# A transformer block on one core: gate logits out of the output projection, the normalised input turned by an exchange through DRAM

## The chip, the cores and the metric

The kernel runs on one core of one Trainium2 chip. The metric is the device time of one execution in microseconds. A core has TensorE (PE, matmuls and transposes through the array), VectorE (DVE), ScalarE (ACT), GpSimd (POOL), and SyncE (SP), which here only issues DMAs; 16 DMA engines move the data.

## The reference

The input is 16 sequences of 256 tokens with 256 features, and one condition vector per sequence.

```python
shift = jax.nn.silu(t) @ W_ada.T + b_ada
h = _ln(x, ln1_g, ln1_b) + shift
qkv = (h @ Wqkv.T).reshape(b, n, 3, H, HD)          # H = 16 heads of HD = 64
q = _ln(q, qn_g, qn_b); k = _ln(k, kn_g, kn_b)      # per head
attn = jax.nn.softmax(q @ k.T / sqrt(HD))
x = x + (attn @ v) @ Wout.T
tok = x.reshape(-1, d)                              # 4096 tokens
gate = jax.nn.softmax(tok @ Wgate.T, axis=-1)       # E = 8 experts
vals, idx = jax.lax.top_k(gate.T, 4096 // E)        # each expert picks 512 tokens
g = _ln(tok[idx], mlp_g, mlp_b)
y = gelu(g @ fc1.T + b1s) @ fc2.T + b2s             # 1024 hidden
tok = tok.at[idx].add(y * vals)
```

## The kernel before

All arithmetic is in float32; a matmul of the program appears as two records in the profile. Every PE step of the attention part works on one sequence b.

**First** (per sequence): the tokens arrive as two tiles of 128 rows. VectorE takes mean and variance (L623, L625), GpSimd the reciprocal square root (L629, L106), VectorE applies both (L635, xn), PE turns the two tiles with four transposes (L659, into PSUM, ph), and ScalarE evicts them with gain and bias (L667) as hT, features on the partitions.

**Group** (six column groups of 512 for q, k and v, by two tiles): PE multiplies hT with the weights (L696, pm). For q and k ScalarE squares (L709), VectorE sums by head (L713), GpSimd takes the power (L106) and VectorE scales (L733, qk). Except in sequence 0 (`DIRECT`), the result is turned without PE: VectorE transposes 32x32 blocks (L765), SP sends them to a DRAM scratch tile (`away`, L772) and fetches them back in another order (`back`, L783), and ScalarE applies gain and bias (L789, L797). Such a pair of DMAs through DRAM is called an exchange.

**Quad** (four per sequence, four heads each): PE scores (L822, sc), VectorE maxima (L830), ScalarE exponentials (L843), GpSimd normalises (L854), and the probabilities are turned: by an exchange (L864 transpose, L872 away, L885 back into prT), or, for the quads in `OFFS`, by PE transposes (L891, pp) and a ScalarE copy (L898). Before the change `OFFS` holds all four quads of sequence 0 and the last two of sequence 15. PE multiplies with v (L910, po), ScalarE evicts (L925, oT).

**Tail** (two tiles per sequence): PE projects oT with `wo` in eight accumulating matmuls (L936, pw); VectorE adds the residual (L943, tok) and normalises it again for the experts; SP stores both to DRAM (L947, L957). For the gate PE transposes tok twice (L962, pg), ScalarE copies it (L968, tokT), PE multiplies with the gate weights (L973, pl) and VectorE copies the 8 logits (L979, gates).

**Routing**: with the gates of sequences 0 to 14, a bitwise search of 30 steps finds each expert's threshold; each step is a VectorE comparison (L1101), a small PE count (L1110, pc) and a VectorE choice (L1125). Sequence 15's last work and filler transposes (L557) stand between the steps. Then the lists of tokens are made (L1154 to L1254).

**Jobs**: 16 expert jobs of 256 tokens each (8 experts, two rounds): load weights (L1211 to L1216), gather tokens, two matmul layers (L1333, L1353), scatter-add to the output.

The order of the instructions up to the first job's end is written out by hand: each step is declared once with its engine, and the list `PLACES` gives every step a number; the steps are issued in the order of these numbers.

```python
def order(self, places):
    assert len(places) == len(self.steps)
    return sorted(range(len(places)), key=lambda k: (places[k], k))
```

Every engine works through its own instructions in that order, and waits at one whose input or buffer isn't ready. SP is one such queue: a DMA that waits there holds those behind it.

Of the kernel before, what the change touches and what calls it, by code (L numbers as in the profile page):

```python
# [9 lines left out]
F32 = mybir.dt.float32  # L10
I32 = mybir.dt.int32
BF16 = mybir.dt.bfloat16
AF = mybir.ActivationFunctionType
# [53 lines left out]
def kernel(  # L67
# [6 lines left out]
    woutT: bass.AP,  # L74
    wgateT: bass.AP,
# [76 lines left out]
    def make_others():  # L152
# [21 lines left out]
    DIRECT, OFFS = (0,), {(b, d) for b in (0, B - 1) for d in range(HP // 2)} - {(B - 1, 0), (B - 1, 1)}  # L174
# [11 lines left out]
        0, 0, 3.75, 4.52, 3.3, 4.02, 4.42, 7.76, 0.23, 0, 8, 9.39, 23.39, 15.62, 11.2, 13.11,  # L186
        20.2, 18.21, 0, 0, 0, 0, 0, 0, 0, 3.5, 4.21, 5.54, 5.02, 5.73, 6.59, 7.1, 7.76, 10.88,
        12.83, 14.5, 15.29, 17.61, 24.11, 24.82, 14.6, 16.55, 19.6, 20.39, 22.79, 26.35, 27.24,
        12.61, 14.56, 17.01, 17.93, 21.59, 25.9, 26.57, 18.4, 20.35, 22.19, 22.98, 25.11, 26.8,
        27.91, 22.38, 24.33, 29.19, 31.14, 27.46, 29.41, 30.12, 30.98, 32.96, 34.54, 35.93, 30.92,  # L190
        32.87, 33.58, 34.37, 36.58, 49.98, 53.03, 35.14, 39.48, 40.19, 43.73, 45.71, 48.98, 49.77,
        37.37, 39.98, 40.79, 41.85, 43.83, 49.5, 51.4, 39.1, 41.05, 47.25, 49.28, 32.65, 34.78,
        36.6, 38.11, 40.83, 41.54, 34.18, 34.97, 39.02, 41.27, 42.03, 37.84, 42.73, 33.67, 35.38,
        37.56, 40.03, 41.71, 42.52, 35.98, 38.52, 40.94, 42.15, 43.01, 39.76, 45.64, 46.88, 43.75,
        44.99, 45.78, 51.95, 55.85, 56.57, 46.91, 50.44, 52.86, 56.29, 57.06, 51.68, 58.63, 44.77,
        46.31, 47.37, 53.77, 61.53, 62.58, 47.51, 52.07, 54.68, 65.43, 66.15, 53.31, 66.89, 68.13,
        56.73, 58.17, 58.96, 65.08, 73.25, 73.97, 61.18, 63.07, 69.75, 75.42, 76.14, 64.31, 80.95,
        57.76, 59.98, 61.13, 63.26, 75.86, 76.63, 59.38, 60.17, 64.17, 78.03, 78.74, 62.99, 79.93,
        82.15, 65.87, 67.71, 68.62, 72.43, 89.64, 90.45, 67.11, 69.58, 71.52, 88.18, 88.9, 71.25,
        92.4, 78.91, 80.39, 81.19, 88.14, 94.44, 95.25, 84.26, 85.77, 89.05, 90.23, 94.21, 87.01,  # L200
        99.51, 101.48, 112.85, 116.83, 117.98, 117.98, 119.21, 119.72, 119.79, 120.23, 125.51,
        126.28, 116.32, 120.15, 122.66, 121.3, 122.16, 123.66, 125.96, 127.43, 132.51, 133.33, 0,
        15.1, 17.17, 27.27, 12.59, 13.3, 24.78, 46.66, 48.33, 50.66, 53.7, 54.41, 55.59, 57.57,
        58.77, 54.12, 56.07, 56.78, 59.35, 61.78, 63.16, 52.39, 54.34, 55.05, 57.47, 60.58, 62.38,
        63.18, 64.54, 67.74, 69.34, 74.46, 61.97, 64.03, 64.74, 65.99, 68.31, 69.1, 69.9, 71.34,
        74.54, 76.14, 80.34, 59.65, 62.09, 67.91, 70.54, 63.7, 65.65, 66.36, 67.87, 69.85, 70.64,
        69.79, 71.74, 72.45, 73.34, 75.32, 76.11, 71.52, 73.47, 74.18, 75.22, 77.32, 78.11, 78.91,
        80.27, 83.47, 85.07, 89.39, 73.69, 75.64, 76.72, 77.51, 79.79, 80.99, 81.79, 83.15, 86.35,
        87.95, 93.36, 76.3, 78.25, 82.84, 87.23, 81.82, 83.66, 84.81, 86.32, 87.38, 83.06, 83.85,
        87.23, 88.59, 86.05, 89.39, 90.75, 93.95, 95.55, 104.14, 88.62, 89.86, 90.94, 93.72,  # L210
        95.37, 90.46, 91.9, 94.63, 95.98, 93.34, 96.78, 98.14, 101.34, 102.94, 108.93, 114.54,
        93.42, 94.77, 95.74, 103.48, 104.54, 96.59, 101.97, 104.39, 106.35, 103.21, 107.15,
        108.51, 111.73, 113.93, 127.28, 98.49, 99.73, 100.52, 105.3, 109.36, 100.33, 102.93,
        106.21, 110.57, 104.17, 111.37, 112.73, 116.16, 118.36, 128.3, 129.49, 105.16, 107.56,
        108.71, 114.78, 117.83, 106.96, 107.75, 112.05, 116.22, 111.78, 122.3, 124.9, 128.1,
        129.97, 139.32, 106.18, 108.76, 111.12, 112.96, 114.39, 108.16, 110.16, 113.87, 115,
        112.55, 115.8, 117.16, 120.7, 122.9, 138.3, 140.41, 109.95, 112.72, 115.03, 120.22,
        125.07, 111.95, 113.58, 119.31, 129.55, 119.04, 130.35, 131.97, 135.17, 136.77, 142.08,
        121.74, 123.27, 124.06, 126.71, 130.68, 123.87, 125.02, 127.62, 128.94, 126.44, 131.48,
        133.17, 136.77, 138.77, 143.1, 145.7, 159.6, 163.6, 164.95, 164.75, 166, 166.55, 173.78,  # L220
        174.91, 176.32, 177.22, 163.07, 167.2, 168.65, 168.35, 170.41, 172.99, 176.77, 179.56,
        180.45, 181.22, 0, 26.23, 27.18, 28.97, 25.71, 26.42, 27.6, 78.47, 79.23, 84.72, 86.73,
        87.99, 89.96, 91.94, 92.73, 86.45, 88.4, 89.2, 91.84, 94.17, 97.19, 90.67, 92.86, 93.57,
        95.54, 97.8, 99, 99.8, 101.16, 104.36, 106.14, 112.08, 95.03, 96.98, 98.4, 99.19, 101.17,
        101.96, 102.94, 104.94, 108.14, 109.74, 115.99, 96.76, 103.89, 107.05, 109.67, 100.53,
        104.88, 105.75, 107.12, 109.97, 115.61, 102.41, 104.38, 105.15, 109, 111.18, 121.15,
        110.97, 113.08, 113.79, 115.69, 118.44, 119.54, 120.34, 121.7, 124.9, 126.5, 132.75,
        120.01, 121.96, 122.67, 123.46, 125.68, 126.61, 127.41, 128.77, 131.97, 134.37, 139.02,
        123.63, 126.94, 129.17, 131.31, 122.76, 127.74, 128.53, 132.16, 133.49, 124.47, 125.98,
        133.07, 134.7, 131.89, 138.37, 140.77, 143.97, 145.57, 155.83, 126.26, 128.34, 130.35,  # L230
        138.22, 139.83, 131.29, 135.85, 139.13, 140.44, 137.09, 141.24, 142.6, 145.8, 147.57,
        154.81, 156.92, 131.49, 132.73, 133.75, 136.4, 148.24, 134.1, 134.89, 137.31, 147.02,
        136.13, 149.04, 150.99, 154.95, 157.79, 171.89, 140.19, 142.03, 142.82, 145.91, 156.57,
        141.43, 143.78, 146.82, 153.56, 145.64, 157.37, 159.79, 162.99, 164.59, 172.91, 175.21,
        141.21, 143.23, 144.74, 154.31, 160.52, 145.04, 149.04, 151.52, 159.91, 150.28, 161.39,
        163.39, 167.05, 168.99, 185.54, 149.31, 150.55, 151.34, 158.04, 161.73, 154.17, 154.96,
        158.95, 162.34, 157.18, 164.59, 166.59, 169.79, 171.39, 184.52, 188.07, 150.33, 152.35,
        157.41, 160.92, 170.74, 154.77, 158.37, 160.01, 169.8, 159.74, 174.92, 177.12, 180.72,
        182.72, 190.02, 156.7, 157.94, 162.28, 165.51, 175.49, 159.14, 161.32, 166.42, 171.95,
        165.2, 176.29, 178.32, 182.68, 185.92, 191.04, 192.13, 198.43, 202.27, 204.54, 203.47,  # L240
        204.66, 207, 215.16, 215.88, 216.4, 217.76, 206.68, 210.37, 212.02, 212.16, 213.19,
        216.86, 213.06, 216.18, 222.5, 223.22, 0, 28.45, 29.46, 48.11, 26.75, 27.94, 48.44,
        131.05, 131.8, 133.11, 137.31, 138.12, 140.04, 142.63, 143.83, 134.84, 136.81, 137.52,
        141.92, 144.44, 146.41, 136.57, 138.52, 139.23, 143.8, 145.81, 147.63, 148.43, 149.79,
        152.99, 154.59, 159.33, 145.85, 147.8, 148.85, 149.64, 151.75, 152.95, 154.59, 156.59,
        159.79, 161.39, 165.59, 143.97, 146.19, 153.08, 155.92, 147.58, 150, 151.15, 152.43,
        155.97, 162.99, 151.2, 153.3, 155.37, 156.16, 158.54, 166.59, 157.72, 160.33, 161.13,
        161.92, 164.6, 165.39, 166.19, 167.79, 171.39, 173.39, 179.86, 166.54, 168.49, 169.2,
        169.99, 172.56, 173.76, 174.56, 175.92, 179.12, 180.72, 184.92, 168.27, 170.22, 174.59,
        176.65, 170, 173.16, 173.95, 178.17, 179.23, 171.35, 172.14, 179.08, 180.61, 177.71,  # L250
        182.32, 184.72, 187.92, 189.52, 195.52, 171.02, 174.37, 178.1, 180.11, 181.38, 176.1,
        177.14, 181.02, 182.59, 179.84, 184.92, 187.92, 191.12, 192.72, 212.04, 214.1, 182.63,
        185.36, 186.15, 193.17, 194.4, 184.76, 187.11, 192.26, 193.79, 190.79, 196.32, 198.54,
        205.4, 207.74, 219.75, 183.65, 190.19, 190.98, 194.08, 195.61, 187.17, 189.06, 194.99,
        196.22, 192.22, 197.02, 199.74, 202.94, 204.54, 218.73, 221.32, 196.54, 198.38, 199.53,
        202.56, 203.88, 197.78, 198.57, 201.65, 203.27, 201.38, 205.04, 206.54, 214.9, 217.74,
# [1455 lines left out]
```

## Time and profile before

| | us |
|---|---|
| median of three runs | 1073.79 (1072.8 to 1074.13) |
| the profiled execution | 1073.31 |
| its span, first to last instruction | 1071.6 |
| PE busy | 1036.4 (97%) |
| VectorE busy | 825.5 (77%) |
| GpSimd busy | 617.2 (58%) |
| ScalarE busy | 589.6 (55%) |
| token transposes on PE (L962), busy | 12.7 |
| input transposes on PE (L659), busy | 10.1 |
| gate products on PE (L973), busy | 17.5 |
| projections on PE (L936), busy | 115.2 |

The mean granted TensorE clock is 0.988. Busy times of PE overlap: a record lasts until its modelled end, and the next has begun by then. In the profile a line such as `pw<-wo,oT` reads "pw is written from wo and oT", with the shape and the number of records; "idle" and "wait" name the engine and line that released the waiting instruction.

### The profile page before, as it was taken

The page shows a single profiled execution, that of the slowest core. Times are in us where ns is not written, and L with a number is a line of the kernel's source. Part 1 is how long each engine was busy: PE and PEld are TensorE (multiplying, and loading weights), DVE is VectorE, ACT ScalarE, POOL GpSimd, SP SyncE. Part 2 cuts the span into 40 slices and gives each one's busy share as a digit, 9 for nine tenths or more (in the row PEclk, how much of TensorE's full clock was granted, in tenths as well). Part 3 has the DMA queues.
Part 4 walks back from the last instruction along what each step waited for, and adds up shares of the span by engine and source line. Part 5 has one row for each costly group of instructions (what it writes and reads, how often), then busy time and mean ns, then how long its engine had stood idle before and what let it go on. Part 6 is the DMA issues. An engine that isn't in the chain of part 4 may idle for free. (4 is left out here: it accounts for less than half of the span.)

```text
span 1071.6 us, 17747 instructions
## 1 busy us (share of the span) xinstructions
PE 1036.4 (97%) x5519; PEld 677.5 (63%) x5519; DVE 825.5 (77%) x2295; ACT 589.6 (55%) x1646; POOL 617.2 (58%) x997
## 2 busy tenths in 40 slices
PE   7899999999999999999999999999788999999996
PEld 4455656555555655556566565666477888888885
DVE  6667888989888898798888888888667588656530
ACT  1577676676666666575766667675503323333231
POOL 3666776778767686667767686675401423343332
PEclk8999999999999999999999999999999999999999
DMA  6014889888987898887888888899430656667772
GB/s 218 1 60 158 272 290 324 290 290 283 308 274 264 285 317 311 289 289 262 287 301 289 290 296 292 291 316 309 167 102 22 184 146 188 197 189 203 232 236 30
DMA packets 169710, 250.53 MB, mean 234 GB/s; under 512 B 9744, under 2 KB 139536, under 8 KB 169616
## 3 DMA queue, kind: packets, MB, share of 16 engines
q1 hardware_dynamic: 161696, 239.11, 65.8%
q0 software_dynamic: 6144, 8.39, 4.3%
q10 hardware_dynamic: 1776, 1.90, 0.5%
q8 instruction: 44, 0.72, 0.3%
q14 instruction: 50, 0.41, 0.1%
HBM read 142.67 MB, written 106.69 MB: 233 GB/s over the span
## 5 line engine op out<-in xcount | busy, mean ns | idle before, releaser
L696 PE MATMUL pm<-wq,hT 128*128 128x512 f32 x768 | 362.1, 609 | 6.7 <-DVE qk L733 2.5
L854 POOL TENSOR_SCALAR pr<-pr,sums 128x256 f32<-128x256 f32 x512 | 238.2, 486 | 97.2 <-DVE sums L850 90.1
L843 ACT ACTIVATE pr<-sc,nmax 128x256 f32<-128x256 f32 x512 | 237.8, 481 | 102.0 <-DVE nmax L830 81.3
L696 PEld LDWEIGHTS pm<-wq,hT 128*128 128x128 f32 x768 | 138.3, 191 | 162.2 <-issue 138.0
L106 POOL TENSOR_TENSOR ss<-ss,neghalf 128x8 f32<-128x8 f32 x128 | 210.7, 1646 | 10.7
L830 DVE TENSOR_REDUCE nmax<-sc 128x2 f32<-128x512 f32 x256 | 165.7, 676 | 13.8 <-PE sc L822 13.1
L864 DVE STREAM_TRANSPOSE pb<-pr 128x512 f32<-128x512 f32 x232 | 154.1, 687 | 7.4 <-POOL pr L854 6.9
L822 PE MATMUL sc<-kT,qT 64*128 64x256 f32 x1024 | 135.2, 394 | 0.0
L910 PE MATMUL po<-prT,v 128*64 128x256 f32 x1024 | 128.8, 389 | 2.7 <-DMA prT<-blocks 2.7
L709 ACT ACTIVATE sq<-pm 128x512 f32<-128x512 f32 x128 | 76.8, 604 | 89.7 <-PE pm L696 87.3
L1370 POOL DMA_INDIRECT out<-y,idx x32 | 50.9, 1592 | 122.7 <-DVE oh L1246 57.1
L822 PEld LDWEIGHTS sc<-kT,qT 64*128 64x128 f32 x1024 | 91.3, 186 | 46.9 <-issue 28.5
L1333 PE MATMUL ph<-xT,w 128*128 128x256 f32 x512 | 116.8, 383 | 0.9 <-ACT xT L1318 0.9
L936 PE MATMUL pw<-wo,oT 128*128 128x256 f32 x512 | 115.2, 381 | 0.0
L1353 PE MATMUL py<-w,hid 128*128 128x256 f32 x512 | 115.1, 380 | 0.0
L910 PEld LDWEIGHTS po<-prT,v 128*64 128x64 f32 x1024 | 66.9, 137 | 68.5 <-issue 19.9
L936 PEld LDWEIGHTS pw<-wo,oT 128*128 128x128 f32 x512 | 96.3, 190 | 21.0 <-issue 6.0
L843 ACT ACTIVATION_READ_ACCUMULATOR pr<-sc,nmax 128x1 f32 x512 | 108.2, 211 | 0.0
L733 DVE TENSOR_TENSOR qk<-pm,ss 128x512 f32<-128x512 f32 x128 | 89.7, 702 | 23.8 <-POOL ss L106 21.5
L1353 PEld LDWEIGHTS py<-w,hid 128*128 128x128 f32 x512 | 96.1, 190 | 13.2
L1333 PEld LDWEIGHTS ph<-xT,w 128*128 128x128 f32 x512 | 95.0, 190 | 14.9 <-ACT xT L1318 2.4
L713 DVE TENSOR_REDUCE ss<-sq 128x8 f32<-128x512 f32 x128 | 85.1, 670 | 22.1 <-ACT sq L709 20.5
(144 smaller groups left out, 1050.6 us busy)
## 6 DMA issues: line engine op xcount, KB each, us to landing
blocks<-pb SPq DMA_DIRECT2D x116, 512.0 KB
prT<-blocks SPq DMA_DIRECT2D x116, 512.0 KB
kblocks<-kb SPq DMA_DIRECT2D x60, 512.0 KB
w<-in_fc2T SPq DMA_DIRECT2D x16, 1024.0 KB
qraw<-kblocks SPq DMA_DIRECT2D x30, 512.0 KB
kT<-kblocks SPq DMA_DIRECT2D x30, 512.0 KB
w<-in_fc1T SPq DMA_DIRECT2D x9, 1024.0 KB
w<-in_fc1Q SPq DMA_DIRECT2D x7, 1024.0 KB
```

Of the source, the lines that this page charges most:

```text
L106: nc.gpsimd.tensor_tensor(dst, src, neghalf[:, : src.shape[1]], ALU.pow)
L696: nc.tensor.matmul(self.pm, hTs[self.b][:, c, bass.ts(self.t, P)], wq[:, c, bass.ts(self.g, GW)], start=(c == 0), stop=(c == DC - 1),)
L733: engine.tensor_tensor(dst, src.rearrange("p (q e d) -> p q e d", q=QB, e=8), by_head(self.ss[:, 1, :]), ALU.mult,)
L822: nc.tensor.matmul(self.sc[i, j][:, t, :], qTs[self.b][rows, hp, bass.ts(t, P)], keys[rows, hp] if whole else keys[rows, hp // 4, hp % 4], ...
L830: nc.vector.tensor_reduce(self.nmax[i, j], self.sc[i, j], AX.X, ALU.max, negate=True)
L843: nc.scalar.activation(dst, src, AF.Exp, bias=self.nmax[i, j][:, t : t + 1], scale=1.0, accum_out=self.sums[i][:, 0, j, t : t + 1],)
L854: nc.gpsimd.tensor_scalar(self.pr[i, j][:, t, :], self.pr[i, j][:, t, :], self.sums[i][:, 1, j, t : t + 1], 1.0, ALU.mult, ALU.mult,)
L864: nc.vector.transpose(self.pb[i][:, :, :, j].rearrange("p k c t n -> p t k c n"), self.pr[i, j].rearrange("p t (k c m) -> p t k c m", c=TB ...
L910: nc.tensor.matmul(self.po[j * HD : (j + 1) * HD, i, :], vs[self.b][:, c, bass.ts(4 * self.d + 2 * i + j, HD)], prT[:, j, c] if (self.b, s ...
L936: nc.tensor.matmul(self.pw, oTs[self.b][:, hp // 2, self.t, hp % 2, :], wo[:, hp, :], start=(hp == 0), stop=(hp == HP - 1),)
L1333: nc.tensor.matmul(self.ph[f], self.w1[:, c, bass.ts(f, P)], self.xT[:, :, c].rearrange("p k i n -> p k (i n)") if self.exchanged else sel ...
L1353: nc.tensor.matmul(self.py[i], self.hid[:, f, bass.ts(i, P)], self.w2[:, f, :], start=(f == 0), stop=(f == FC - 1),)
```

## The change

**Gate.** With tok = x + o Wout.T, the logits are tok Wgate.T = x Wgate.T + o (Wgate Wout).T. A new step `Fold` loads Wout once more, multiplies it with the gate weights on PE and writes the result as 8 more columns of `wo`, so that the projection is 264 columns wide. Two small matmuls add the part of x, for which x is loaded a second time, transposed on the host (`xT`, one buffer, one load per sequence). The token transposes, their copy and the separate gate product are gone; the logits are copied out of pw.

**Input.** Except in sequence 0 (`XDIRECT`) the normalised input is turned by an exchange: ScalarE applies mean and reciprocal deviation (with an offset that GpSimd makes), VectorE transposes 32x32 blocks, SP sends and fetches, ScalarE applies gain and bias. The weights are permuted on the host to match.

**Quads.** (0, 2) and (0, 3) leave `OFFS`: their probabilities go by exchange.

**Weights of the first jobs.** Their loads come behind the first step of the routing (`"turned"`). **Order.** `PLACES` is new as a whole, and the costs written beside the steps are changed (they have no effect in the kernel, which takes only the order from `PLACES`).

```diff
-    DIRECT, OFFS = (0,), {(b, d) for b in (0, B - 1) for d in range(HP // 2)} - {(B - 1, 0), (B - 1, 1)}
+    DIRECT, OFFS = (0,), {(b, d) for b in (0, B - 1) for d in range(HP // 2)} - {(B - 1, 0), (B - 1, 1), (0, 2), (0, 3)}
+    EXCHANGED = (0, 1, 2, 3)
+    XDIRECT = (0,)
...
-        wo = attw.tile([P, HP, D], F32, name="wo")
+        wo = attw.tile([P, HP, D + E], F32, name="wo")
...
+        def load_xT(b):
+            xTs[b] = seq.tile([P, DC, N], F32, tag="xT", bufs=1, name=f"xT{b}")
+            nc.sync.dma_start(
+                xTs[b], xT[:, b * N : (b + 1) * N].rearrange("(c p) n -> p c n", p=P)
+            )
+
+        class Fold:
+            def load(self):
+                self.w = seq.tile([P, DC, H * HD], F32, tag="oT", bufs=2, name="wout")
+                nc.sync.dma_start(self.w, wout.rearrange("(c p) f -> p c f", p=P))
+
+            def product(self):
+                self.pf = ps.tile([P, HP, E], F32, tag="mm", bufs=3, name="pf")
+                for hp in range(HP):
+                    for c in range(DC):
+                        nc.tensor.matmul(
+                            self.pf[:, hp], self.w[:, c, bass.ts(hp, P)], wg[:, c],
+                            start=(c == 0), stop=(c == DC - 1),
+                        )
+
+            def evict(self):
+                nc.scalar.copy(wo[:, :, D:], self.pf)
...
+            def offset(self):
+                nc.gpsimd.tensor_scalar(
+                    self.rs[:, 0:1], self.mv[:, 0:1], self.rs[:, 1:2], -1.0, ALU.mult, ALU.mult
+                )
...
+                    nc.scalar.activation(
+                        dst, src, AF.Identity, bias=self.rs[:, 0:1], scale=self.rs[:, 1:2]
+                    )
...
+            def turn(self, t):
+                if t == 0:
+                    self.xb = work.tile([P, QB, DC, TB, SQ], F32, tag="qk", bufs=3, name="xb")
+                nc.vector.transpose(
...
+            def away(self):
+                self.blocks = dram.tile([QB, SQ, QB, P], F32, tag="xblocks", bufs=2, name="xblocks")
...
+            def back(self):
+                self.raw = work.tile([P, QB, DC, TB, SQ], F32, tag="sq", bufs=2, name="xraw")
...
+            def affine(self):
+                b = self.b
+                hTs[b] = seq.tile([P, DC, N], F32, tag="hT", name=f"hT{b}")
+                for c in range(DC):
+                    nc.scalar.activation(
+                        hTs[b][:, c].rearrange("p (t k n) -> p k t n", t=TB, k=QB),
+                        self.raw[:, :, c], AF.Identity,
...
-            def project(self, a=0, b=HP):
-                if a == 0:
-                    self.pw = ps.tile([P, D], F32, tag="mm", bufs=3, name="pw")
-                for hp in range(a, b):
+            def project(self):
+                self.pw = ps.tile([P, D + E], F32, tag="mm", bufs=3, name="pw")
+                for hp in range(HP):
                     nc.tensor.matmul(
                         self.pw, oTs[self.b][:, hp // 2, self.t, hp % 2, :], wo[:, hp, :],
-                        start=(hp == 0), stop=(hp == HP - 1),
+                        start=(hp == 0), stop=False,
+                    )
+                for c in range(DC):
+                    nc.tensor.matmul(
+                        self.pw[:, D:], xTs[self.b][:, c, bass.ts(self.t, P)], wg[:, c, :],
+                        start=False, stop=(c == DC - 1),
                     )
...
-            def transposes(self):
-                self.pg = ps.tile([P, D], F32, tag="mm", bufs=3, name="pg")
...
-            def evict(self):
-                self.tokT = work.tile([P, D], F32, tag="tokT", name="tokT")
...
-            def gate(self):
-                self.pl = ps.tile([P, E], F32, tag="po", name="pl")
...
-                nc.vector.tensor_copy(gates[:, self.n, :], self.pl)
+                nc.vector.tensor_copy(gates[:, self.n, :], self.pw[:, D:])
...
-        at(-999, "ACT", 0.3, later_loads)
+        at(-999, "ACT", 0.3, later_loads, ["sT"])
...
-            at(ROUTE + 60 + n * 80, "SP", 1.5, jobs[n].load, (), [("w", n)], [("oT", B + n), ("v", B + n)], lag=6.0)
+            at(ROUTE + 60 + n * 80, "SP", 1.5, jobs[n].load, ["turned"], [("w", n)], [("oT", B + n), ("v", B + n)], lag=6.0)
```

## The prediction

> **What bounds the kernel now.** I read the busy times and slices of the page first, to see where which engine is full.
>
> ```profile
> span 1071.6 us, 17747 instructions
> ...
> PE 1036.4 (97%) x5519; PEld 677.5 (63%) x5519; DVE 825.5 (77%) x2295; ACT 589.6 (55%) x1646; POOL 617.2 (58%) x997
> ...
> PE   7899999999999999999999999999788999999996
> ...
> DMA  6014889888987898887888888899430656667772
> ```
>
> TensorE (PE) is full from slice 3 to 28, has a dent at slices 29 to 31 (the routing) and is full again in the expert stage; the DMA engines are nearly as full in the attention stage, at 8 or 9 tenths. A busy PE is modelled, so I asked next for the whole attention stage as one window (PE, PEld, DVE, ACT, POOL busy, then clock, DMA share, GB/s), and for what made PE wait inside it.
>
> ```profile
> 55.00:757.00 702.00, 701.35 (x3436) 404.04 (x3434) 598.16 (x1193) 472.41 (x1396) 493.25 (x849) 1.00 0.82 279
> ```
>
> ```profile
> PE pl L973 <- DVE gates L979: 0.4, 1, 0.4
> PE pm L696 <- ACT hT L667: 0.2, 1, 0.2
> ```
>
> These two lines are all the PE waits of 702 us: 0.6 us. VectorE has 104 us to spare there, ScalarE 230, GpSimd 209. So in this stage a microsecond of PE work is a microsecond of the span, until something else takes over. Prices must be steps of PE, not means of overlapping records, so I read them from the timeline of PE as the distance from one start to the next.
>
> ```profile
> 448.05 3.72 PE L936 MATMUL pw<-wo,oT 128*128 128x256 f32 x16
> 451.61 1.88 PE L696 MATMUL pm<-wq,hT 128*128 128x512 f32 x4
> 453.32 0.38 PE L962 MATMUL pg<-ident,tok 128*128 128x128 f32 x2
> 453.54 1.88 PE L696 MATMUL pm<-wq,hT 128*128 128x512 f32 x4
> 455.26 0.51 PE L973 MATMUL pl<-wg,tokT 128*128 128x8 f32 x4
> 455.70 2.00 PE L822 MATMUL sc<-kT,qT 64*128 64x256 f32 x16
> ...
> 459.50 0.66 PE L659 MATMUL ph<-ident,xn 128*128 128x128 f32 x4
> 460.00 1.88 PE L696 MATMUL pm<-wq,hT 128*128 128x512 f32 x4
> ```
>
> One projection (pw) takes 3.56 us, the two token transposes (pg) 0.22 here and 0.28 at the other tile of this sequence, a gate product (pl) 0.44, the four input transposes (ph) 0.50.
>
> **The change, part by part.** All on PE first, over 16 sequences of two tiles.
>
> Removed: pg, 32 tiles by 0.27 us (12.7 us busy in the groups over 64 records is 0.40, but records overlap; the starts over the whole stage give 0.22 to 0.28, mean 0.27): -8.7. ph, 15 sequences by 0.50: -7.5 (sequence 0 keeps them). Two quads of sequence 0 go from PE transposes (pp) to the exchange: 32 transposes; 16 of them start at 48.18 and the next step at 50.02, so 0.115 each: -3.7. Their four exchanges meet a DMA at 0.16 to 0.45 (slices 3 and 4), and VectorE's eight transposes of 0.69 its gaps there: 0.
>
> Added: the projection's rows go from 256 to 264 columns, 3.56 x 8/256 = 0.11 per tile, 32 tiles: +3.5 (ends: 0, if 8 columns hide in the issue, and 7, if they cost double). The gate product stays, as two matmuls with x transposed instead of the token transposed: same shapes, same 0.44, so 0 (it loses its own waits, 0.4 us, and its tokT copy). The fold is 16 matmuls with 8 columns, two records each, 32 at pl's 0.11 a record: +3.5 once, at the start, where PE has 11 us of gaps before 54 us (the first two slices); between 0 (in a gap) and 7 (with a slow clock: the first slice had 0.80). I take all of 3.5.
>
> Sum on PE: -8.7 - 7.5 - 3.7 + 3.5 + 3.5 = -12.9. The last sequence's two tiles are projected in the routing stage, where PE is not the bound: 2 x (0.27 - 0.11) = 0.3 is not on the path. **-12.6 us.** I compared the two written-out orders as lists: up to the last projection of sequence 14, which the routing waits for, both put the same 192 QKV groups, 126 score steps and 120 products on PE, so no work moves across that point, and PE changes mode about as often (255 and 254 times, some 0.1 us each).
>
> Other engines, per sequence. VectorE: two applies of 0.43 leave, two 128x256 transposes of 0.45 come (the row xb<-xg, L1296): nothing. ScalarE: two tokT copies (0.38) and two evictions (0.58) leave, two applies (0.38 to 0.58 by the 128x256 rows) and two affines (0.59) come: +0.2 of 15 free. GpSimd: two offsets of 0.2: +0.4 of 13 free. SP issues three more DMAs, 0.3 to 0.4 us each. All lie under PE. If that cover were gone they would cost 0.6 a sequence.
>
> DMA is the tight one. In 107 to 750 us:
>
> ```profile
> q1 hardware_dynamic: 124550, 187.34, 85.9%
> ```
>
> That is 552 us of 16 engines for 187 MB, 2.95 us per MB. The first projections of sequences 0 and 14 start at 120.50 and 743.68, 44.5 us per sequence, so 38.2 us of DMA in each. New are the away and the back of the normalised input and x transposed, 256 KB each, 0.79 MB: 2.3 us, together 40.5. PE's period falls by 0.54 + 0.50 - 0.22 = 0.82 to 43.7. DMA goes from 86% to 93%. Does PE start to wait there? The nearest rows:
>
> ```profile
> 160.74:187.53 26.79, 26.79 (x128) 16.55 (x127) 23.51 (x51) 17.62 (x53) 18.45 (x34) 1.00 0.97 324
> 375.06:401.85 26.79, 26.79 (x132) 14.36 (x132) 25.23 (x47) 18.41 (x52) 22.85 (x36) 1.00 0.94 317
> 735.00:763.00 28.00, 25.52 (x167) 17.86 (x165) 21.41 (x56) 19.24 (x67) 15.30 (x34) 1.00 0.95 331
> ```
>
> At 0.97 and 0.94 in mid-stage PE never idled; at 0.95 at the end, with little other work to put before a late product, it did. Ends: 0, and (below) +25. Mid-stage is the nearer row: I take +1.
>
> The Trainium skill's page "DMA: Bandwidth & Descriptors" (Bandwidth, Rules for kernel authors) speaks against small transfers: batch to 1 MiB or more, 0.95 us for 64 KB and 6.15 us for 1 MB. On a line between them, as an estimate, 256 KB takes 2.0 us and the three 6.0, and DMA would need 44.2 us per sequence, over PE's 43.7. The trace disagrees so far: its transfers of 512 KB and less cost 2.95 us per MB.
>
> The added waits. The x-transposed load has one buffer, so SP waits at it until the sequence before is projected, and behind it on SP stand the aways and backs of the next quads; the order puts it right behind that projection, so I count 0. The input's exchange adds two DMA trips before the QKV groups; the nearest rows are those of the expert stage, in the chain of waits:
>
> ```profile
> 967.85 2.62 DMA xblocks<-xb
> 970.53 2.84 DMA xT<-xblocks
> ```
>
> 5.5 us, more under load; the new order has the affine at least one full QKV step and mostly several ahead of its first reader, so 0. It borrows a qk and an sq buffer for that time, which PE's groups need; at 3 and 2 buffers against some 7 us in 43.7 I count 0 and leave it to the +1. The wait of the early loads for the silu changes nothing: they are issued at 7.30, behind it (4.24), already.
>
> End of attention and routing. With pg and pl gone there is less to put between the last exchanges of sequence 14 and its products: a prT wait, +1.5 (0 to 4). On the other side the first job's weights, issued at 741.62 to 744.21 in the middle of those exchanges, now go behind the routing's first transpose. The waits there:
>
> ```profile
> PE pc L1110 <- DVE reach L1101: 5.9, 11, 0.8
> PE po L910 <- DMA prT<-blocks: 2.7, 3, 1.1
> ```
>
> Of the 2.7 I take -1. The second job's load now comes first, so the first job's may be the one that waits for a buffer of the last projection, as the second one's does now (issued at 794.15, when that projection ends; its bytes are through 10 us later). That projection now stands just before the totals, and from the totals (804.37) to the first expert matmul (819.97) are 15.6 us: it lands under the routing's end, 0; without those 5 us to spare it would cost up to that. The last projection moves from between two routing steps to just before the totals: +0.5.
>
> Total: -12.6 + 1 + 1.5 - 1 + 0.5 = **-10.6 us**. The profiled execution took 1073.31 us (span 1071.6 and 1.7 around it), which gives 1062.7; the median of the three runs is 0.5 above it, so I forecast 1063.
>
> **Rivals.**
> (1) Part of the gain is absorbed: the start (chains, not PE, set it, and the fold and ScalarE's applies for sequences 1 to 4 sit in it) gives back 3 to 5 us and the others 2 more: 1069. For it: PE has those 11 us of gaps, which no PE saving touches. Against: only the fold and one sequence's transposes are there.
> (2) Slower: the exchanges come late to their products. Place: po<-prT; price: the three waits at 759 to 765 us, 0.9 each; a sequence saves 0.82, so it decides from one late product in eight per sequence. At three, 14 x 2.7 = 38 less the 10.6: 1100; at two, 1088. For it: DMA at 93%, one queue on SP, one more wait in it. Against: 0.97 was borne for 27 us without a wait.
> (3) DMA occupancy is the bound: if each of the three new transfers takes 2.0 us of the 16 engines (three quarters of the landing times above), DMA needs 44.2 a sequence, 0.5 over PE's period: 14 x 0.5 = 7 of the gain is lost, 1070. The Trainium skill's rule above gives this time. Against it stands 2.95 us per MB.
> (4) It comes to nothing: the 8 extra columns and the fold cost double (+7) and prT waits of 4 more, the end's upper bound, take the rest: 1073.
>
> **How the numbers follow.** Forecast 0.66 (own range 1058 to 1067); (1) 0.10; (3) 0.05; (2) 0.15; (4) 0.04. About 0.2% (2.1 us) is what a measurement here can tell from no change. Faster: 0.66 + 0.10 + 0.05 = 0.81; same 0.04; slower 0.15. Low end: fold in the gaps (-3.5) and all prT waits gone (-1.7): 1057. High end: (1), (3), (4) and the beginning of (2), one late product in each sequence, 14 x 0.9 = 12.6 on the 1062.7: 1076.
>
> **What would show it.** Right: PE work in the attention stage 12 to 13 us less, pg gone, ph with 4 records, pw near 3.67 plus 0.44 a tile; PE waits on prT under 3 us there; DMA 0.90 to 0.95; sequence 14 projected some 11 us earlier. Wrong: rows PE po <- DMA prT with tens of waits, or pw at more than 4.2 us a tile with its gate part, or a first expert matmul not earlier than 812.

## The result

The changed kernel takes 1078.22 us (median of 20 runs, 1074.11 to 1083.36), the kernel before 1073.72 (20 runs, 1071.31 to 1077.81): ratio 1.0044, 95% interval 1.0033 to 1.0054, so 4.5 us slower. In a later comparison the ratio was 1.0027 (1.0013 to 1.0041, 10 runs). The forecast was 1063.

The profiled execution took 1075.04 us, near the lower end of those runs, with a span of 1073.3 against 1071.6 of before. So the profile shows 1.7 of the 4.5 us. First the page after: busy PE, then its 40 slices, then those of the DMA engines.

```profile
span 1073.3 us, 17620 instructions
...
PE   6899999999999999999999999998979999999996
...
DMA  7017899999999888999898899997603656666772
```

DMA has moved up to 8 and 9, as expected. The dent of the routing is a slice earlier, but not followed by anything that ends earlier. The attention stage as one window and PE's longest waits in it (engine and line, what it waited for, us in total, times, longest):

```profile
55.00:757.00 702.00, 696.77 (x3312) 391.40 (x3311) 599.39 (x1199) 473.83 (x1386) 503.74 (x880) 1.00 0.88 299
```

```profile
PE sc L910 <- ACT kT L885: 1.8, 1, 1.8
PE sc L910 <- DVE nmax L918: 1.7, 1, 1.7
...
```

With three shorter rows the waits come to 5.2 us, from 0.6, and none of them is the prT wait that the prediction watched for. The prices of the steps and the DMA share came out near what was worked out: a projection with its gate part takes 3.66 + 0.37, and the queue holds the 16 engines for 90.3% of 107 to 750 us (85.9% before, 93% forecast).

```profile
442.55 3.83 PE L1023 MATMUL pw<-wo,oT 128*128 128x264 f32 x16
446.21 0.51 PE L1028 MATMUL pw<-wg,xT 128*128 128x8 f32 x4
446.58 1.96 PE L784 MATMUL pm<-wq,hT 128*128 128x512 f32 x4
```

Where the time went is seen at the two ends of the stage. At the start, from the timelines of before and then of after, ScalarE's issues of QKV weights (before all three, after the last two) and PE's first QKV step:

```profile
7.74 3.11 ACTq L590 DMA_DIRECT2D wq<-in_wqkvT  x3
...
11.60 7.64 PE L696 MATMUL pm<-wq,hT 128*128 128x512 f32 x12 [0.51 <-ACT hT L667]
```

```profile
7.70 1.75 SPq L583 DMA_DIRECT2D wout<-in_wout  x1
9.99 0.37 ACTq L627 DMA_DIRECT2D wq<-in_wqkvT  x1
16.36 0.37 ACTq L627 DMA_DIRECT2D wq<-in_wqkvT  x1
...
17.48 6.99 PE L784 MATMUL pm<-wq,hT 128*128 128x512 f32 x12 [6.90 <-ACT hT L755]
```

SP sends Wout (1 MB) and the first x transposed out at 7.7 and 10.7 us, behind the first loads. The order names a need for the fold's load, the third sequence's statistics, but only its plan knows of it: the DMA itself reads and overwrites nothing that is in use, so SP doesn't wait for it. From the start of its first weight issue to the end of its third ScalarE needs 8.14 us instead of 3.11, and the eviction of hT behind them on ScalarE comes 5.9 us later, with it the first QKV step.

An issue by itself takes 0.37 to 0.51 us; the time goes by ahead of the third, 6.0 us after the second. There ScalarE waits for a semaphore, the counter that tells of a DMA's landing. In the records of these traces the first DMAs of SP and ScalarE use eight semaphores together, and from the ninth on an issue starts 0.02 us or more after the DMA that had its semaphore before has landed. Before, the third weight load has the semaphore of another weight load, landed at 10.45 us, and is issued at 10.47. After, the two added loads take two semaphores, the third weight load gets that of `wo` (1 MB), landed at 16.34, and is issued at 16.36.

At the other end, PE's timeline after, where little but sequence 15's scores is left:

```profile
734.35 2.12 PE L910 MATMUL sc<-kT,qT 64*128 64x256 f32 x16
738.15 0.70 PE L910 MATMUL sc<-kT,qT 64*128 64x256 f32 x2 [1.67 <-DVE nmax L918]
739.06 1.13 PE L910 MATMUL sc<-kT,qT 64*128 64x256 f32 x6 [0.21 <-ACT pr L931]
742.01 2.08 PE L910 MATMUL sc<-kT,qT 64*128 64x256 f32 x8 [1.82 <-ACT kT L885]
744.02 3.68 PE L998 MATMUL po<-prT,v 128*64 128x256 f32 x16
```

The last QKV matmul starts at 729.0, where before has one at 738.0. Then score steps stand one behind the other, PE waits for VectorE's maxima, for ScalarE's exponentials and longest for kT, which ScalarE finishes at 741.96 behind eight exponentials, and two product steps that take 1.88 us elsewhere take 3.6: the granted clock is 0.81 in 736:744 and 0.77 in 744:752, where before has 1.00 in both.

The span's difference by stages (start of the first QKV step; end of the last gate product that the routing needs; the routing's first transpose; first expert matmul), with the kernels of the experiments:

| kernel | QKV | gates | routing | experts | span | median | ratio to before (95%) |
|---|---|---|---|---|---|---|---|
| before | 11.6 | 755.0 | 760.3 | 820.0 | 1071.6 | 1073.7 | 1 |
| after | 17.5 | 756.8 | 760.9 | 820.2 | 1073.3 | 1078.2 | 1.0044 (1.0033 to 1.0054) |
| e1_hold | 11.5 | 752.0 | 756.1 | 814.5 | 1067.5 | 1073.9 | 0.9999 (0.9982 to 1.0016) |
| e2_before_early | 17.3 | 758.4 | 762.9 | 823.3 | 1075.2 | 1076.4 | 1.0026 (1.0014 to 1.0038) |
| f1_fill_hole | 11.7 | 751.7 | 755.8 | 815.8 | 1068.0 | 1069.9 | 0.9964 (0.9950 to 0.9978) |
| f3_no_exchange_early | 10.8 | 757.5 | 761.7 | 822.3 | 1074.9 | 1076.6 | 1.0033 (1.0022 to 1.0044) |
| f4_end_order | 10.9 | 746.3 | 749.4 | 811.4 | 1064.6 | 1066.4 | 0.9947 (0.9926 to 0.9968) |
| g1_split_last | 11.4 | 750.1 | 753.2 | 808.7 | 1061.6 | 1062.6 | 0.9919 (0.9887 to 0.9950) |
| g2_weights_back | 12.2 | 751.4 | 755.4 | 820.5 | 1075.0 | 1074.8 | 1.0015 (0.9998 to 1.0031) |

The ratios are to runs of before on the same chip (1072.6 to 1074.0 there). The stages are of one execution each; e1, profiled twice, differs by 4 us in them, so a stage's difference of a few us is only believed where the medians say the same.

### The profile page after: what moved, and what is told of

Same layout as the page of the kernel before. It is cut to its first block, busy times and chain, and to the rows that moved or that the text cites. A ratio compares the mean times of both kernels' runs of the same rounds, so it can differ in the third digit from the quotient of the medians.

```text
span 1073.3 us, 17620 instructions
## 1 busy us (share of the span) xinstructions
PE 1032.2 (96%) x5395; PEld 668.4 (62%) x5395; DVE 825.4 (77%) x2303; ACT 590.6 (55%) x1637; POOL 625.5 (58%) x1027
## 5 line engine op out<-in xcount | busy, mean ns | idle before, releaser
L108 POOL TENSOR_TENSOR ss<-ss,neghalf 128x8 f32<-128x8 f32 x128 | 210.9, 1648 | 10.7
L952 DVE STREAM_TRANSPOSE pb<-pr 128x512 f32<-128x512 f32 x240 | 158.0, 685 | 10.3 <-POOL pr L942 5.6
L998 PE MATMUL po<-prT,v 128*64 128x256 f32 x1024 | 131.0, 391 | 0.1
L1023 PE MATMUL pw<-wo,oT 128*128 128x264 f32 x512 | 122.4, 393 | 0.0
L1406 PE MATMUL ph<-xT,w 128*128 128x256 f32 x512 | 116.8, 383 | 2.4 <-ACT xT L1391 2.4
L1406 PEld LDWEIGHTS ph<-xT,w 128*128 128x128 f32 x512 | 95.0, 190 | 16.4 <-ACT xT L1391 3.7
```

The lines of the kernel that those rows point to most:

```text
L108: nc.gpsimd.tensor_tensor(dst, src, neghalf[:, : src.shape[1]], ALU.pow)
L952: nc.vector.transpose(self.pb[i][:, :, :, j].rearrange("p k c t n -> p t k c n"), self.pr[i, j].rearrange("p t (k c m) -> p t k c m", c=TB ...
L998: nc.tensor.matmul(self.po[j * HD : (j + 1) * HD, i, :], vs[self.b][:, c, bass.ts(4 * self.d + 2 * i + j, HD)], prT[:, j, c] if (self.b, s ...
L1023: nc.tensor.matmul(self.pw, oTs[self.b][:, hp // 2, self.t, hp % 2, :], wo[:, hp, :], start=(hp == 0), stop=False,)
L1406: nc.tensor.matmul(self.ph[f], self.w1[:, c, bass.ts(f, P)], self.xT[:, :, c].rearrange("p k i n -> p k (i n)") if self.exchanged else sel ...
```

## The experiments

**The start.** The theory: the early 1.25 MB is what delays the first QKV step. One kernel holds it back, the other gives it to the kernel before.

```diff
 class Fold: def load(self):
     self.w = seq.tile([P, DC, H * HD], F32, tag="oT", bufs=2, name="wout")
+    nc.vector.memset(self.w[:, :, 0:1], 0.0)
     nc.sync.dma_start(self.w, ...)
```

> The changed kernel, with one VectorE memset into the tile of Wout ahead of its load, at the load's place in the order, so that the 1 MB really waits until some 20 us and does not go out behind the first loads. Theory 1 (the early 1.25 MB fills the queues, ScalarE stands 5 us longer in issuing its three wq loads and hT comes late): first QKV matmul back from 17.5 to 11.6 +- 0.4 us, ScalarE's three issues back from 8.1 to about 3 us, time 5 to 6 us less than the changed kernel's 1078.2, so 1072 to 1073.5. Rival (the start is late because of the new order or of the wait for the silu): first QKV matmul stays at 17 to 17.5, time 1077 to 1079.

Measured: first QKV step at 11.49, median 1073.9, 0.4 us over the expected range. ScalarE's issues end at 10.75, as those of before do (10.85). The third weight load again has the semaphore of another weight load (landed at 10.30, issued at 10.32).

```diff
 for b in (3, 4): load_x(b)          # before.py, last_loads
+early = seq.tile([P, DC, H * HD], F32, tag="oT", ...); nc.sync.dma_start(early, wout...)
+early = seq.tile([P, DC, H * HD], F32, tag="oT", ...); nc.sync.dma_start(early[:, :, :N], xT...)
```

> The kernel before, with the loads of Wout (1 MB) and of x transposed of sequence 0 (0.25 MB) put behind its first loads on SP, into tiles that nobody reads; nothing else changed. Theory 1: first QKV matmul at 16 to 17.5 instead of 11.6 us, time 4 to 6 us over the 1073.7 of before: 1077.7 to 1079.7. Rival (the late start belongs to the order): 1073.5 to 1074.5, first QKV matmul at 11.6 to 12.

Measured: first QKV step at 17.30, as in the changed kernel; median 1076.4, 1.3 us under the expected range, because of the 5.7 us lost at the first step 2.3 are won back on the way to the gates. Both say the same: the early loads cost 2.4 to 4.3 us, in either order. The rival falls. Here too the third weight load stands behind `wo`: `wo` is issued at 4.38, the view of its tile gives

```profile
L604 SPq DMA_DIRECT2D wo<-in_woutT x1: 538/538/538, 4.4 to 4.4; - x1
DMA to landing us min/median/max: 11.8/11.8/11.8
```

so it lands at 16.16, and the third weight load is issued at 16.18. So the loads do not simply fill the queues, as the theory had it. In e1 `wo` lands at 14.90: by that, as an estimate, some 4.5 of the 5.9 us come from the change of semaphore (10.47 to 14.9) and the rest from the added bytes. No run takes the two apart.

**The middle: the input's exchange, and the fold alone.** Between the stage's ends PE has many more gaps of some 0.1 us. Theory 2 put them down to the exchange.

```diff
-XDIRECT = (0,)
+XDIRECT = tuple(range(B))    # with e1's memset; e4: ph 0.9 us ahead of the first QKV step in the order, f3: 3.6
```

> e1 with the input's exchange undone: VectorE applies, PE transposes (ph, 15 x 0.50) and ScalarE evicts as before, just ahead of each sequence's first QKV group; the rest of the new order stands. Theory 2 (the exchange makes the small gaps, some 11 us): +7.5 of ph, -9 to -11 of gaps: 1 to 4 us less than e1, about 1070. Rival 2b (the new order makes the gaps, or the fold): +7 to +8 over e1, about 1080.

Measured: 1091.2, ratio 1.0159 (1.0125 to 1.0193): neither. The order that I wrote put the eviction too close to its reader:

```profile
PE pm L750 <- ACT hT L721: 8.3, 13, 0.7
```

So it prices a bad place, not the exchange, and was run again with more room.

> e4 again, the input's exchange undone on top of e1, but with the four transposes and the eviction put 3.6 us of the order ahead of the first QKV group (more for three sequences), so that nothing waits for hT. Theory 2b (the exchange is worth the 15 x 0.50 = 7.5 us of its transposes and costs nothing in waits): 7 to 9 us over e1. Rival 2 (the exchange gives part of it back in small waits): 3 to 6 us over e1.

Measured: 1076.6. By the ratios that is 3.6 us over e1 (some 2 either way): rival 2. Where the other half of the 7.5 us went is not settled. Against e1's first profile the small gaps are not the exchange's: the distances from start to start, summed by tile from the first QKV step to the gates, are the same in f3 and e1 (QKV 358.1 and 358.0, scores 131.4 and 131.1, products 116.8 and 117.6), though f3 has no exchange of the input and its 15 sequences' transposes take 7.85. But that was e1's fastest run. Its second profile (below), near its median as f3's is, has 360.5, 132.5 and 118.5, 5.2 us more than f3 in these three, so by that one the exchange does give back part of its gain in small waits.

```diff
-OFFS = ... - {(B - 1, 0), (B - 1, 1), (0, 2), (0, 3)};  XDIRECT = (0,);  PLACES = those of after
+OFFS = ... - {(B - 1, 0), (B - 1, 1)};  XDIRECT = tuple(range(B));  PLACES = those of before, step by step
```

> The fold alone, in the order of before: gate columns in the output projection, x transposed loaded behind each sequence's last projection, Wout's load held back as in e1, the fold's product at 46 us of the order; the input transposes stay on PE, the two quads of sequence 0 keep theirs, the first jobs' weights stay where they were. By the steps of PE: token transposes -8.2, gate products -1.8, 8 columns +3.2, fold +3.6, so -3.2: 1070.5. Theory 2 (the small gaps of some 0.1 us on PE, 16 us before and 28 us after the change, come from the input's exchange and its closer waits): gaps stay at 16 to 18 us and the time is 1069.5 to 1071.5. Rival 2a (they come from the x transposed and the DMA traffic it adds): gaps over 22 us, time 1074 or more.

Measured: 1090.8, ratio 1.0156 (1.0140 to 1.0172): theory 2 missed by far, and rival 2a's "1074 or more" holds only as a number. The steps have the forecast prices, but the order of before without its token transposes and gate products runs into waits, the first line in 55:757, the second in 757:782:

```profile
PE pm L749 <- DVE qk L786: 4.1, 6, 1.1
```

```profile
PE po L963 <- DMA prT<-blocks: 4.8, 4, 1.7
```

The removed steps had covered other chains. A hand-written order with steps taken out is another order, so this run doesn't price the fold.

**The hole at the end of attention.** Theory 3: what the middle gains is lost in the hole at 732 to 746 us. f1 only fills it, f4 takes it away.

```diff
+at(729.75, "PE", 1.7, partial(fill_mm, 16), ...)   # fill_mm: fill with its tile in "mm"
+at(734.3, "PE", 1.3, partial(fill_mm, 12), ...)
+at(736.0, "PE", 0.9, partial(fill_mm, 8), ...)
```

> e1 with 36 identity transposes of no use put on PE into the hole at the end of attention (16 behind the first score step of sequence 15's second quad, 12 behind the next, 8 behind the one after; 0.11 us each). In e1's profile PE idles there from 732 to 740 us and its granted clock falls to 0.62 in 736:744. Theory 3 (the hole costs twice: the waits, and a lower clock afterwards whose place and length vary from run to run, which is why the median of e1 lies 4.6 us over its profiled run): clock 1.00 in those windows, the product behind the hole back from 3.06 to 1.95 us, median 2 to 4 us under e1's 1073.9, spread of the runs narrower than e1's 8.6 us. Rival 3a (the low clock is harmless, the scores wait for ScalarE anyway): median within 1 us of e1.

Measured: 1069.9, 4.0 under e1's median (3.8 by the ratios), with 36 matmuls of no use added; spread 5.9 us. One window of e1, then of f1 (columns as above):

```profile
736.00:744.00 8.00, 6.74 (x35) 3.58 (x34) 5.15 (x11) 5.67 (x21) 4.49 (x10) 0.62 0.49 165
```

```profile
736.00:744.00 8.00, 7.64 (x60) 5.27 (x57) 5.78 (x13) 6.71 (x25) 4.69 (x11) 1.00 0.63 213
```

The product behind the hole is back from 3.06 to 1.95 us. So the low clock is not harmless, and rival 3a falls. How much of the 4.0 it is, the profiles leave open: from sequence 13's last projection to sequence 14's first f1 takes 25.1 us, e1 26.2 and, in its second profile, 27.0. The Trainium skill's page "TensorE: Matmul & The Clock Gate" (Part 1, What's actually happening) says that PE falls to half its clock after an idle window of about 3.4 us, and that this window runs free of the kernel; the trace agrees with a fall, since 0.62 lies between half and full, but not with that length: e1's longest idle stretch in the hole is 1.67 us. No run here shows that the window runs free.

f4 gives all engines another order from 688 us on. On PE, from the first projection of sequence 13:

```diff
-pw13.0 pm pm sc14.3 po pm po sc14.3 pw13.1 pm pm po po sc15.0 po po sc15.0 sc15.1 (hole) sc15.1 (hole) sc15.2
+pw13.0 pm pm pm sc14.3 sc14.3 po po pw13.1 sc15.0 po po pm sc15.0 sc15.1 pm po sc15.1 po sc15.2
```

> e1 with the last 60 us of attention in another order on all engines: the last projection of sequence 13, the two last value groups and the scores of sequence 15 are spread so that PE never waits for a score buffer; in the order's own times the holes of 3.7 and 0.9 us at 730 us become one of 1.0 and the routing's first transpose comes 4.2 us earlier. Theory 3 (the hole at the end of attention is where the middle's gain goes): routing's first transpose 4 to 7 us earlier than e1's 756.1, no clock under 0.9 between 728 and 756 us, median 4 to 7 us under e1: 1067 to 1070. Rival 3b (the end is set by the exponentials and exchanges of sequence 15, whatever the order of PE): routing's start within 1.5 us of e1's, 1072.5 to 1074.

Measured: 1066.4, 7.5 under e1 by the medians (of six runs) and 5.6 by the ratios (some 3 either way); the routing's first transpose at 749.4 against 756.1; clock 1.00 from 728 to 752. Rival 3b falls: the end was set by the order.

**The routing.** In f4 the last projection stands between the last threshold count and the totals. g1 cuts both projections of sequence 15 into pieces behind sixteen counts.

```diff
-def project(self):
+def project(self, a=0, z=HP):      # one hp per piece; the gate part with the last
-at(p, "PE", 4.07, a.project, ...)
+for z in range(HP): at(p + z, "PE", 0.45 if z < HP - 1 else 0.9, partial(a.project, z, z + 1), ...)   # b == 15
```

> f4 with the two projections of sequence 15 cut into eight pieces of 0.45 us each (the last with the gate part 0.9), one piece behind each of the sixteen threshold counts from 20 to 5 of the routing, where PE is free for some 0.9 us per count; the tail of the first of them on VectorE and the first job's weights behind it move along. In f4 they stand as blocks: 4.1 us between two counts, where a count takes 1.0, and between the last count (789.8) and the totals (795.9), 6.1 us where before had 1.0. Theory 4 (the last projection moved ahead of the totals costs 3 to 5 us and not 0.5): last count to first expert matmul back from 21.7 to 16 to 18 us, first expert matmul 5 to 7 us earlier than f4's 811.4, median 1060 to 1062. Rival 4a (VectorE's chain or the weights' landing set the start of the experts): 1065 to 1067.

Measured: 1062.6. The medians of f4 and g1 stand on six runs each and their intervals overlap; the profiles are clearer, f4's last count and what follows, then g1's:

```profile
789.78 0.16 PE L1182 MATMUL pc<-cnt,twice 128*128 128x1 bf16 x1
789.80 5.85 PE L1022 MATMUL pw<-wo,oT 128*128 128x264 f32 x16
...
795.85 0.16 PE L1226 MATMUL po<-tot,below 128*128 128x1 bf16 x1
```

```profile
779.52 0.18 PE L1187 MATMUL pc<-cnt,twice 128*128 128x1 bf16 x1
779.56 0.69 PE L1025 MATMUL pw<-wo,oT 128*128 128x264 f32 x2
...
780.54 0.16 PE L1187 MATMUL pc<-cnt,twice 128*128 128x1 bf16 x1
```

Between the two counts stand the piece and a fill, and the second still comes 1.02 us after the first: the piece costs the chain next to nothing. From the routing's first transpose to the first expert matmul f4 takes 62.1 us, g1 55.5, from the last count on 21.7 and 18.4. Theory 4 has the mechanism right and each of its numbers a little too good: 18.4 instead of 16 to 18, a median of 1062.6 instead of 1060 to 1062, and a first expert matmul only 2.7 us earlier than f4's instead of 5 to 7, since this execution reached the routing 3.8 us later. By their ratios to before, g1 is faster than before and after.

**The first jobs' weights.**

```diff
-790.7  SP  load of job 0's weights        # place in f4's order
+735.1  SP  load of job 0's weights        # ahead of the away of sequence 15's second quad, as in before
-773.7  SP  load of job 1's weights
+790.7  SP  load of job 1's weights
```

> f4 with the first job's weights (2 MB) loaded where before loads them, amid the last exchanges of sequence 14 and 15 on SP, and the second job's behind the last projection, so undoing that part of the change. Theory (the 2 MB delay the exchanges behind them): waits of PE on prT in 728 to 790 us of 2 to 5 us instead of 0.2, median 1 to 4 us over f4's 1066.4. Rival (the transfers find room, as the prediction's -1 nearly says): within 1 us of f4.

Measured: 1074.8, 8.3 over f4 (7.3 by the ratios), twice what the theory allowed. PE's waits in 728:790, f4 and then g2:

```profile
PE sc L909 <- ACT kT L884: 1.1, 1, 1.1
PE po L997 <- DMA prT<-blocks: 0.2, 1, 0.2
```

```profile
PE po L997 <- DMA prT<-blocks: 3.9, 3, 2.8
PE sc L909 <- ACT kT L884: 2.1, 1, 2.1
```

So 4.7 us of waits come back; 3.0 more lie in the routing (65.1 us instead of 62.1 to the first expert matmul). The move is worth it in f4's order; in the changed kernel itself it wasn't undone.

**A second profile.** The changed kernel's runs spread over 9 us, e1's over 8.6, and e1's first profile was its fastest run.

> e1 again for one look at a profile. e1's first profile was of its fastest run (1069.3, median 1073.9). Theory 3 (a typical run loses some 4 us more of clock behind the hole at 732 to 740 us, and, later, in the routing): if this run takes 1073 or more, the windows between 736 and 816 us show 3 to 5 us more lost clock than the first profile's, and the stages before 730 us are the same within 1 us. Rival: the difference is spread over the whole attention stage.

> The changed kernel again for one look at a profile, for the same question: at 1077 us or more the loss beyond the profiled 1075.0 lies behind the hole and in the routing (theory 3), or is spread (rival).

Measured: e1 at 1073.6 us. It is behind its first profile by 1.8 us when sequence 0 is projected, by 3.3 at sequence 13, by 4.1 at the routing and 4.3 at the end. That is the rival: lost a little everywhere, and the hole adds only 0.8. So theory 3 holds for the hole, but not as the reason for the spread. The changed kernel, at 1076.3 and so short of the 1077 that its question needed, follows its first profile within 0.5 us up to the routing. Why these orders spread more than before stays open.

> The changed kernel once more, on the same chip as the others. Theory 3: its profile shows PE idle for 4 to 6 us between 732 and 746 us and a clock under 0.9 in some 8 us there, and, where its time is nearer the median of 1078 than the first profile's 1075, more clock lost there or at the start of the experts; first QKV matmul at 17 to 18 us again. Rival: no clock lost, the time lies elsewhere.

Measured: 1075.9; in its profile (1073.75) the first QKV step stands at 16.4, below the expected 17 to 18, the clock is 0.72 in 736:744 and 0.85 in 744:752, and the hole is the same. Here `wo` lands at 15.29 and the third weight load is issued at 15.31.

## Why the prediction was wrong

**PE's work: right in its parts, 2.6 us too large in sum.** By tile, in distances from start to start up to the gates: token transposes -8.2 (forecast -8.7, of 32 tiles where this sum has 30), input transposes -7.5 (-7.5), pp -4.0 (-3.7), columns +3.2 (+3.5), fold +3.6 (+3.5), gate products -1.8 (0). But these -14.7 are not what the work became less. What was wrong is the price of a removed step. In all traces here a run of score steps takes 0.863 a step and 0.201 once, a run of products 0.863 a step and 0.151 once, and a QKV step beside such a run 0.093 to 0.104 more. Both orders change between these kinds equally often (254 and 252 times), as the prediction counted, but part of those costs stood in the 0.27 of pg and the 0.50 of ph (four transposes are 4 x 0.109 = 0.436). A removed step leaves it to its neighbours: 32 x 0.05 + 15 x 0.065 = 2.6. With every step at these prices the work up to the gates is 728.4 us before and 718.4 after: -10.0 in place of -12.6. Most of it shows in the QKV steps, as many as before, which by these prices cost 4.3 us more. This is worked out from the traces; no run tests it by itself.

**The start: the failed step.** "The fold ... I take all of 3.5" priced its matmuls and left out its 1 MB. The prediction followed the plan's need and not the instruction, which has none, so the load had no price at all. What the runs show in its place: the added loads move ScalarE's third weight load to the semaphore of the 1 MB `wo`, and the eviction of hT waits behind it on ScalarE. It costs 5.9 us at the first QKV step, 2.4 to 4.3 in the end. Rival (1) had the place and the size, 3 to 5 us, but by another mechanism (the fold's matmuls and ScalarE's applies), and a chance of 0.10.

**The end of attention: the other failed step.** It was given "a prT wait, +1.5 (0 to 4)". The row says 7.7 us: 6.0 over price in the score run from 734 us and 1.7 in the products behind it, none of it for prT. The two orders were compared by counts of steps up to the last projection of sequence 14. Compared by their own times they show it: in the new one the score step at 728.82 (0.87 long) is followed on PE by one at 733.37. f4 shows what it is worth, 7.5 us of median (5.6 by the ratios), the clock behind the hole included.

**Sum for the profiled execution, up to the gates:** first QKV step +5.9, work -10.0, gate products -1.0 below the common price, waits from there to 50 us -3.1 (10.4 instead of 13.5), the middle +2.1, the end +7.7: +1.6, measured +1.8. The middle's +1 (measured 2.1) was near in size by luck, since it was meant for prT waits and none came; nor did rivals (2) and (3): no prT wait at 90% DMA. The added 10.96 MB took 28.3 us of the 16 engines, 0.68 us per 256 KB. The 2.0 us per transfer estimated from the Trainium skill's page "DMA: Bandwidth & Descriptors" is not what such a transfer takes of the 16 engines here. Of the prediction's own signs, "a first expert matmul not earlier than 812" came (820.2), and sequence 14 was projected 5.0 us later, not 11 earlier.

**The rest.** The last projection ahead of the totals was put at +0.5: before, the two projections stretch their counts by 6.3 us together, after, one stretches its counts by 3.9 and the other delays the totals by 4.4, so +2.0. The moved weights were put at -1; in f4's order they are worth 8.3 (7.3 by the ratios). The experts take 253.2 instead of 251.6 us, which nothing in the prediction says and no run explains.

## What to carry to other kernels

A need that stands only in a plan doesn't hold a DMA back: where a load is to come late, its tile must depend on something late. DMAs that share semaphores wait for each other: an added load can put another engine's issue, and the compute instructions behind it, behind the landing of a large transfer. When a full engine is relieved, look at the order's own times for the place where its work runs out first (here the last scores), since the gain ends there and the clock behind the gap takes more; spreading the independent steps that were left was worth 5.6 to 7.5 us of 1074 here. A step's price read beside changes of matmul shape holds part of their cost, which stays when the step goes.

## What was not expected of the hardware

An engine can stand for long between two issues though each issue takes 0.37 us: ScalarE stood 6.0 us ahead of its third weight load in the changed kernel, 1.4 before and 0.09 in e1, with the 16 DMA engines at a share of 1.07 to 1.08 in 8 to 16 us each time. So it was not the load on the engines that differed, but the transfer whose landing the issue waited for. And a granted clock of 0.62 to 0.85 goes with a stretch in which PE is still busy half of the time (4.29 of 8 us in 736:744 of the changed kernel), with no idle stretch longer than 1.82 us.
